# Output projection of images 1 to 3: reordering pixels in TensorE's read of y, or in VectorE's read of PSUM

## The chip, the cores and the metric

The kernel runs on one NeuronCore of a Trainium2 chip. A core has a matrix engine (TensorE, PE in the profile; its weight loads are PEld), VectorE (DVE), ScalarE (ACT), GpSimd (POOL), SyncE (SP, which issues most DMAs), 16 DMA engines, an on-chip memory SBUF, and PSUM, the memory that TensorE writes its results to, in banks of 128 partitions x 512 fp32. [...] The metric is the device time of one execution in microseconds; lower is better.

## The reference, cut to what matters

The input is x, 4 images of 96 channels x 128 x 128 pixels, fp32. Two layers follow one another, each with a residual sum:

```
x = x + L0(group_norm(x))     # layer 0: a four-direction selective scan over 192 inner channels
x = x + L1(group_norm(x))     # layer 1: convolutions whose weights come from an attention product
```

Layer 0 ends in what the change concerns. ym is the sum of the four scans' outputs, 192 channels for each pixel:

```
mu  = yn.mean(-1);  var = yn.var(-1)                       # over the 192 channels of a pixel
yn  = (yn - mu) * rsqrt(var + 1e-5) * ln_w + ln_b
out = einsum('bdhw,cd->bchw', yn, out_w) + out_b           # back to 96 channels
```

Layer 1 begins with a group norm of x + out, so the mean and variance of each channel over all pixels are needed before it starts.

## The kernel before, in words

The program runs in phases. First it projects and convolves x for all four images; beside this run the selective scans (L735 to L854), written to memory as `yms`. Then `ssm_output` (L923) runs for each image: it normalizes, projects and adds the residual, and stores `xnew`. `split_norm` then makes two maps from `xnew`, and the attention of layer 1 follows.

`ssm_output` takes an image in 16 chunks `c` of 1024 pixels (`SN`), each in two halves `h` of 512 (`CH`). Its loop has 18 steps; in each, chunk c is begun (square and sums), chunk c-1 is in the middle (the inverse deviation), and chunk c-2 is finished. The pieces:

- `load_y` (L938): a DMA brings y, 2 x 96 channels x 1024 pixels; three buffers.
- `squares` and `sums` (L942, L949): ScalarE squares y; TensorE sums y and its squares over the channels.
- `rows`, `inverse`, `roots`, `back` (L961 to L987): the sums are copied out of PSUM, spread by small DMAs over 8 partitions (`mq`), turned into 1/sqrt(var + eps), and written to memory (`rd`).
- `spread_out` (L995): a DMA from GpSimd's queue reads `rd` back into `r`, the same row for 96 partitions. ScalarE adds the output bias to the residual `xr` (L1046).
- `projected` (L1005): TensorE multiplies y by `outws`, the output weights with the norm's scale and the mean's removal folded in, into a PSUM bank `po`. fp32 makes two TensorE instructions of each of the two products for a half, so a half has four.
- `scaled`: VectorE multiplies `po` by `r` (L1012), GpSimd adds `xr` (L1015 for images 1 to 3, L1018 for image 0), and VectorE takes the statistics (L1019). A DMA stores the chunk in `xnew` (L1056).

**Pixel order.** Image 0 keeps the pixels of a row in order. Images 1 to 3 (`turned`) store each row of 128 pixels by column mod 4: first the 32 columns 0, 4, 8, ..., then 1, 5, 9, ..., and so on, since the later phases read pixels that way. `turned_view` (L1237) is the view that reads a row in pixel order as if it were stored so: 32 elements at a step of four fp32 (16 bytes), four times. `back` already writes the inverse deviations in the turned order, so `r` is turned. The residual `xr` is in pixel order and is read by GpSimd through the view. In the kernel before, TensorE reads y (its moving operand) through the view too, and `po` is turned.

**The order of work.** Image 0's `ssm_output` runs beside the end of the scans. That of image 1 runs beside `direct_maps` (image 0's convolutions, L2095), and those of images 2 and 3 beside the attention of the image before (`products`, L1469 and L1484; `Taps`, L1635 and L1745). Two generators are woven together by `co_run` (L290): each piece of the main one has a cost, and the other is advanced by as much cost times a pace. For the phases up to the last scan the order of emission is pinned; after it the scheduler orders the instructions. For images 1 to 3 `ssm_output` has two rotating PSUM banks (`psr`), shared by `po` and the sums.

Of the kernel before, what the change touches and what calls it, by code (L numbers as in the profile page):

```python
# [20 lines left out]
CH = 512  # L21
# [9 lines left out]
TW = 4  # L31
NP = TW + 2
TN = W // TW
# [35 lines left out]
def kernel(  # L69
# [26 lines left out]
    nc = tc.nc  # L96
# [184 lines left out]
    def part(ps, *shape):  # L281
        n = 1
        for d in shape[1:]:
            n *= d
        t = bank(ps)[: shape[0], :n]
        return t if len(shape) == 2 else t.rearrange("p (a b) -> p a b", b=shape[2])
# [636 lines left out]
    def ssm_output(b, yms, xnew, stats, ps, side, turned):  # L923
# [5 lines left out]
        with tc.tile_pool(name="c2", bufs=2, side=side) as p2:  # L929
# [3 lines left out]
            ys, sums_of, near, made = {}, {}, {}, {}  # L933
# [64 lines left out]
            def projected(c, h):  # L998
                po = part(ps, C, CH)
                for j in range(2):  # L1000
                    rhs, to = ys[c][:, j, bass.ts(h, CH)], po
                    if turned:
                        rhs = turned_view(rhs)
                        to = po.rearrange("p (h j t) -> p h j t", t=TN, j=TW)
                    nc.tensor.matmul(  # L1005
                        to, lhsT=outws[:, j], rhs=rhs, start=(j == 0), stop=(j == 1)
                    )
                return po

            def scaled(c, h, po):  # L1010
                xr, r = (t[:, bass.ts(h, CH)] for t in near[c])
                nc.vector.tensor_mul(r, po, r)  # L1012
                if turned:
                    v = r.rearrange("p (h j t) -> p h j t", t=TN, j=TW)
                    nc.gpsimd.tensor_add(v, v, turned_view(xr))  # L1015
                    xr = r
                else:
                    nc.gpsimd.tensor_add(xr, r, xr)  # L1018
                nc.vector.bn_stats(stats[:, 2 * c + h], xr)  # L1019

# [3 lines left out]
            for c in range(NS + 2):  # L1024
                new, old = c < NS, c - 2 if c >= 2 else None
                mid = c - 1 if 1 <= c <= NS else None
                if old is not None:
                    po = projected(old, 0)
# [6 lines left out]
                if old is not None:  # L1035
                    scaled(old, 0, po)
                    po = projected(old, 1)
                    ys.pop(old)
# [10 lines left out]
                if old is not None:  # L1049
                    scaled(old, 1, po)  # L1050
                    load_y(c + 1)
# [185 lines left out]
    def turned_view(v):  # L1237

        return v.rearrange("p (h t j) -> p h j t", t=TN, j=TW)
# [1074 lines left out]
    with tc.tile_pool(name="wp", bufs=1, side="left") as wp:  # L2314
# [7 lines left out]
        for images, pace in (([0], 0.25), ([1], 0.75), ([2, 3], 1.35)):  # L2322
            left = projections(images, weights, stats, wp, psl)
            if images[0] == 0:
# [15 lines left out]
                wdt, wbc, outws, outbs = got  # L2340
# [134 lines left out]
```

## Time and profile before

| | us |
|---|---|
| median of 3 runs | 6757.1 (6746.1 to 6758.7) |
| the profiled execution | 6750.3 |
| its span, first to last instruction | 6748.6 |
| busy: TensorE | 5562.2 (82%) |
| busy: VectorE | 4895.1 (73%) |
| busy: ScalarE | 3810.3 (56%) |
| busy: GpSimd | 3441.7 (51%) |
| mean granted TensorE clock | 0.880 of full speed |

The busy shares are means over phases with different limits. In the slices of the page the span is cut in 40 parts of 168.7 us; each digit is a busy share in tenths, and PEclk is the clock that TensorE was granted, in tenths of full speed. `ssm_output` runs from about 2110 to 2370 us for image 0, 3290 to 3600 for image 1, 4050 to 4400 for image 2 and 4960 to 5290 for image 3. A row of the page's groups reads: line, engine, operation, tiles written and read, shape, count; busy time and mean ns of one; idle time of the engine in front of it and what ended that. In a table of stretches each row has the stretch's bounds and length, then each engine's busy us and its number of instructions, the granted clock, the share of DMA time and GB/s. In a timeline a row has the start, the length of a run of like instructions, the engine, the line, and the count.

### The profile page before, as it was taken

Reading aid. Unit: us, or ns where it says so; the run is one execution under the profiler, and the core shown is the slowest. Engines: PE = TensorE matmul, PEld = TensorE weight load, DVE = VectorE, ACT = ScalarE, POOL = GpSimd, SP = SyncE. Lnnn points to the kernel's source line nnn. Section 1 sums busy time; section 2 is a strip of 40 time slices with the busy share of each in tenths; the row PEclk is TensorE's granted clock in tenths of the full one; section 3 lists DMA queues with packets and bytes.
Section 4 is the critical chain, followed back from the end, with each engine's and each line's share of the span. In section 5 each row is a group of like instructions: output and inputs, shape, how many; then the busy total and the mean of one; then the engine's idle time right before and its main releaser. Section 6 shows DMA issues by size and latency. Waiting matters only on the chain. (4 is left out here: it accounts for less than half of the span.)

```text
span 6748.6 us, 76538 instructions
## 1 busy us (share of the span) xinstructions
PE 5562.2 (82%) x23256; PEld 2361.2 (35%) x23256; DVE 4895.1 (73%) x7737; ACT 3810.3 (56%) x4751; POOL 3441.7 (51%) x2683
## 2 busy tenths in 40 slices
PE   6889978878886628999996679977899877878986
PEld 2333323322221104444332243444333454335652
DVE  3247879989896578889646884488874687987657
ACT  1257768777875576676424453475543664544552
POOL 2236758879796438879422353456123475023410
PEclk9999989989997659999997788888988887999997
DMA  7666777866866666766665765555765555865454
GB/s 163 172 159 177 200 216 198 224 177 171 224 180 166 181 191 191 215 182 175 195 163 157 204 166 152 141 150 146 208 189 150 147 147 148 228 181 139 106 146 146
DMA packets 882102, 1176.27 MB, mean 174 GB/s; under 512 B 215230, under 2 KB 740102, under 8 KB 869212
## 3 DMA queue, kind: packets, MB, share of 16 engines
q1 hardware_dynamic: 858076, 1116.43, 61.1%
q0 software_dynamic: 16208, 38.42, 2.0%
q10 hardware_dynamic: 7408, 16.53, 0.8%
q8 instruction: 187, 3.06, 0.2%
q14 instruction: 223, 1.83, 0.1%
HBM read 766.61 MB, written 334.57 MB: 163 GB/s over the span
## 5 line engine op out<-in xcount | busy, mean ns | idle before, releaser
L621 PE MATMUL bank<-y,wp 128*128 128x512 f32 (+3 forms) x3584 | 1320.4, 626 | 81.6 <-DMA y<-y 33.4
L854 POOL TENSOR_TENSOR y<-y,dl 128x1024 f32<-128x1024 f32 x384 | 1054.2, 2745 | 264.1 <-DVE dl L846 232.5
L821 POOL TENSOR_TENSOR dl<-dl,u 128x1024 f32<-128x1024 f32 x384 | 1007.6, 2624 | 223.5 <-ACT dA L797 123.2
L842 DVE TENSOR_TENSOR_SCAN dA<-dA,pBC 128x512 f32<-128x512 f32 x768 | 981.5, 1278 | 30.8
L1469 PE MATMUL two<-ya,wd 128*64 128x192 f32 (+3 forms) x2376 | 601.1, 433 | 172.0 <-ACT odd L1540 98.0
L735 PE MATMUL pBC<-xr,wbc 60*128 60x512 bf16 (+1 forms) x1536 | 455.7, 401 | 329.8 <-DVE dA L842 257.7
L621 PEld LDWEIGHTS bank<-y,wp 128*128 128x128 f32 (+3 forms) x3584 | 459.1, 169 | 753.1 <-issue 657.0
L846 DVE TENSOR_TENSOR dl<-dA,pBC 128x512 f32<-128x512 f32 x768 | 528.2, 688 | 262.3 <-PE pBC L735 189.0
L2095 PE MATMUL bank<-y,wn 128*128 128x384 f32 (+5 forms) x2408 | 683.0, 509 | 36.7 <-DMA y<-x1d 10.7
L1903 ACT COPY yb<-ya 64x768 f32<-64x768 f32 (+1 forms) x660 | 538.1, 815 | 199.2 <-PE two L1469 151.5
L664 ACT ACTIVATE dl<-pd,dtb 128x512 f32<-128x512 f32 x768 | 486.3, 684 | 181.7 <-PE pd L735 172.1
L1469 PE MATMUL two<-yb,wd 128*64 128x192 f32 (+3 forms) x2376 | 575.0, 416 | 0.0
L825 DVE TENSOR_TENSOR pBC<-dl,pBC 128x512 f32<-128x512 f32 x768 | 527.6, 687 | 9.4 <-POOL dl L821 8.5
L1005 PE MATMUL bank<-y,outws 96*96 96x512 f32 x512 | 455.2, 1025 | 1.8 <-DVE r L1012 1.1
L2095 PEld LDWEIGHTS bank<-y,wn 128*128 128x128 f32 (+3 forms) x2408 | 311.8, 169 | 355.4 <-issue 198.8
L1973 POOL COPY own<-ring 32x512 f32<-32x512 f32 (+1 forms) x198 | 218.2, 1137 | 399.0 <-DVE ring L1562 330.1
L797 ACT ACTIVATE dA<-dl,negA 128x1024 f32<-128x1024 f32 x384 | 420.3, 1141 | 2.3
L1469 PEld LDWEIGHTS two<-ya,wd 128*64 128x64 f32 (+1 forms) x2376 | 272.1, 175 | 400.5 <-issue 106.7
L664 ACT ACT_TABLE_LOAD x245 | 314.3, 1283 | 103.3 <-PE pd L735 95.9
L735 PEld LDWEIGHTS <-wbc 60*128 60x128 bf16 (+1 forms) x1536 | 103.3, 96 | 765.8 <-issue 751.8
L1469 PEld LDWEIGHTS two<-yb,wd 128*64 128x64 f32 (+1 forms) x2376 | 298.8, 175 | 160.3 <-issue 52.5
L1469 PE MATMUL two<-ya,wa 128*96 128x384 f32 (+1 forms) x528 | 230.5, 520 | 132.9 <-DMA wd<-wd 86.7
(308 smaller groups left out, 9665.7 us busy)
## 6 DMA issues: line engine op xcount, KB each, us to landing
u<-zb SPq DMA_DIRECT2D x192, 1024.0 KB
yms<-y SPq DMA_DIRECT2D x96, 512.0 KB
y<-yms SPq DMA_DIRECT2D x64, 768.0 KB
xn<-xnew SPq DMA_DIRECT2D x128, 384.0 KB
ya<-vp SPq DMA_DIRECT2D x120, 336.0 KB
y<-y SPq DMA_DIRECT2D x128, 258.2 KB
zb<-z SPq DMA_DIRECT2D x64, 512.0 KB
ya<-x1p SPq DMA_DIRECT2D x90, 336.0 KB
```

Source lines behind the costliest of these rows:

```text
L621: nc.tensor.matmul(blocks(pz[p:e]), lhsT=ws[k][:, d, c : c + e - p], rhs=window(ys[k], at, d, n), start=(i == 0), stop=(i == len(terms) - 1),)
L664: nc.scalar.activation(dst, src, AF.Softplus, bias=bias)
L735: nc.tensor.matmul(p, lhsT=w[rows], rhs=xr[rows, at : at + CH], start=True, stop=True)
L821: nc.gpsimd.tensor_mul(t, t, u_view(n))
L825: nc.vector.tensor_mul(p, live[n]["dl"][:, bass.ts(half, CH)], p)
L842: nc.vector.tensor_tensor_scan(h, h, p, init, ALU.mult, ALU.add)
L846: nc.vector.tensor_mul(live[n]["dl"][:, sl], live[n]["dA"][:, sl], live[n]["C", half])
L854: nc.gpsimd.tensor_add(v, v, t.rearrange("p (a b) -> p a b", b=W))
L1005: nc.tensor.matmul(to, lhsT=outws[:, j], rhs=rhs, start=(j == 0), stop=(j == 1))
L1469: nc.tensor.matmul(of(to[p:e], r), lhsT=w[:, i, c : c + e - p], rhs=tiles(t[k][PAIR[i]][:, SLOT[i]], o, r), start=(k == 0), stop=False,)
L1903: nc.scalar.copy(yb[k][64 * h - 64 : 64 * h, :, :n], ya[k][0:64, :, h * TN : h * TN + n])
L2095: nc.tensor.matmul(pc[p:e, :n].rearrange("p (h w) -> p h w", w=W), lhsT=w[:, c : c + e - p], rhs=v[:, :, 0:W], start=(i == 0), stop=(i == ...
```

## The change

For images 1 to 3, TensorE reads y in pixel order, as for image 0, so `po` is in pixel order. VectorE's multiplication then reads `po` through `turned_view` and writes `r` in place, in turned order. GpSimd's addition and all that follows is as before. Image 0's instructions are unchanged.

```
             def projected(c, h):
                 po = part(ps, C, CH)
                 for j in range(2):
-                    rhs, to = ys[c][:, j, bass.ts(h, CH)], po
-                    if turned:
-                        rhs = turned_view(rhs)
-                        to = po.rearrange("p (h j t) -> p h j t", t=TN, j=TW)
                     nc.tensor.matmul(
-                        to, lhsT=outws[:, j], rhs=rhs, start=(j == 0), stop=(j == 1)
+                        po,
+                        lhsT=outws[:, j],
+                        rhs=ys[c][:, j, bass.ts(h, CH)],
+                        start=(j == 0),
+                        stop=(j == 1),
                     )
                 return po

             def scaled(c, h, po):
                 xr, r = (t[:, bass.ts(h, CH)] for t in near[c])
-                nc.vector.tensor_mul(r, po, r)
                 if turned:
                     v = r.rearrange("p (h j t) -> p h j t", t=TN, j=TW)
+                    nc.vector.tensor_mul(v, turned_view(po), v)
                     nc.gpsimd.tensor_add(v, v, turned_view(xr))
                     xr = r
                 else:
+                    nc.vector.tensor_mul(r, po, r)
                     nc.gpsimd.tensor_add(xr, r, xr)
                 nc.vector.bn_stats(stats[:, 2 * c + h], xr)
```

`turned_view`, which both use, is unchanged:

```
    def turned_view(v):
        return v.rearrange("p (h t j) -> p h j t", t=TN, j=TW)
```

More of the change, by code (lines that the diff above doesn't have):

```diff
@@ L1000, in projected @@
                 for j in range(2):
[L1001 to L1004, printed above, removed]
                     nc.tensor.matmul(
-                        to, lhsT=outws[:, j], rhs=rhs, start=(j == 0), stop=(j == 1)
+                        po,
+                        lhsT=outws[:, j],
+                        rhs=ys[c][:, j, bass.ts(h, CH)],
+                        start=(j == 0),
+                        stop=(j == 1),
                     )
@@ L1011, in scaled @@
                 xr, r = (t[:, bass.ts(h, CH)] for t in near[c])
-                nc.vector.tensor_mul(r, po, r)
                 if turned:
                     v = r.rearrange("p (h j t) -> p h j t", t=TN, j=TW)
+                    nc.vector.tensor_mul(v, turned_view(po), v)
                     nc.gpsimd.tensor_add(v, v, turned_view(xr))
@@ L1017, in scaled @@
                 else:
+                    nc.vector.tensor_mul(r, po, r)
                     nc.gpsimd.tensor_add(xr, r, xr)
```

## The prediction

> **What bounds the kernel now.** I read the page's engine totals first, then the slices, then the stretches in which the changed lines run, and last the single instructions.
>
> ```profile
> PE   6889978878886628999996679977899877878986
> PEclk9999989989997659999997788888988887999997
> ...
> L1005 PE MATMUL bank<-y,outws 96*96 96x512 f32 x512 | 455.2, 1025 | 1.8 <-DVE r L1012 1.1
> ```
>
> Over the whole span no engine is full (TensorE 82%), so the stretch decides. L1005 is the projection: 512 instructions, two per matrix product, of which 128 belong to image 0 and 384 to images 1 to 3. TensorE was idle for only 1.8 us in front of all of them. The next table is busy time by stretch: image 0's normalization, those of images 1, 2 and 3, then (a second answer) a dense stretch of other work.
>
> ```profile
> core 0: us, PE busy (x) PEld busy (x) DVE busy (x) ACT busy (x) POOL busy (x), PEclk, DMA share, GB/s
> 2110.00:2370.00 260.00, 178.06 (x457) 42.17 (x450) 131.34 (x205) 142.20 (x157) 114.91 (x89) 0.67 0.64 182
> 3290.00:3600.00 310.00, 301.08 (x902) 97.94 (x901) 133.89 (x323) 84.22 (x119) 71.33 (x109) 0.93 0.60 160
> 4050.00:4400.00 350.00, 339.64 (x1442) 136.64 (x1442) 162.32 (x323) 144.90 (x190) 134.16 (x165) 0.88 0.55 146
> 4960.00:5290.00 330.00, 319.56 (x1254) 119.42 (x1255) 166.92 (x300) 131.49 (x168) 126.35 (x152) 0.88 0.56 152
> ...
> 2800.00:3250.00 450.00, 414.73 (x1782) 188.03 (x1781) 393.68 (x480) 317.44 (x402) 371.32 (x143) 0.97 0.65 191
> ```
>
> In the three stretches of images 1 to 3, 990 us together, TensorE is busy for 960 us (97%), VectorE for 463, ScalarE for 361, GpSimd for 332; the DMA share is below 0.61. TensorE is the bound there. How much of it the strided projection takes, and whether it is on the chain:
>
> ```profile
> 3290.00:3600.00 310.00, 122.57 (x128) 20.32 (x128) 0.93 0.60 160
> 4050.00:4400.00 350.00, 122.23 (x128) 22.57 (x128) 0.88 0.55 146
> 4960.00:5290.00 330.00, 122.77 (x128) 21.51 (x128) 0.88 0.56 152
> ```
>
> That is 368 us. The chain of waits, cut to 4990 to 5300 us, gives line L1005 34.9%, its largest share. Last, a run of eight of these matmuls in order of time: two of image 0 (contiguous read), then one of image 3 (strided read).
>
> ```profile
> 2253.79 6.80 PE L1005 MATMUL bank<-y,outws 96*96 96x512 f32 x8
> ...
> 2264.13 3.67 PE L1005 MATMUL bank<-y,outws 96*96 96x512 f32 x8
> ...
> 5059.19 7.42 PE L1005 MATMUL bank<-y,outws 96*96 96x512 f32 x8
> ```
>
> Same line, weights and shape. A single matmul lasts about 0.17 us longer than its turn, so one turn is (3.67 - 0.17)/8 = 0.437 us contiguous and (7.42 - 0.17)/8 = 0.906 us strided. The run of 6.80 us is contiguous at half clock: 0.83 us. Strided turns are 0.90 us in both states of the clock.
>
> [...] this trace's clock records in these stretches are 0.5 or 1.0 alone.
>
> **The change part by part.** As built, the changed program has the same instructions in the same order on all five engines, so nothing is moved past a queue and no DMA is added or removed.
>
> *Matmul reads.* 384 instructions go from 0.90 us (346 us in sum) to 0.437 us at full clock (168 us): 178 us less at full clock, but only 384 x 0.05 at half clock. The rest of TensorE's work in the stretches is 960 - 346 = 614 us at a mean clock of 0.896, or 550 us of full-clock work. So the three stretches take 718/(k s) us, where k is the granted clock and s the share in which TensorE is busy. Now they take 990; the change gains 990 - 718/(k s). The output was already written in contiguous order through its view, so that edit costs nothing.
>
> *The share s.* Idle is now 30 us. Part of the strided time is cover: in each half step the squares' sums (L949) wait for ScalarE's square (L942, 1.05 us), with two projection matmuls between (2.02 us at 3402.03). With about 1.05 us of cover left some 0.3 us shows; 96 halves make 29 us. VectorE waited 22.9 us in all for the DMA of r; a shorter step (990/54 = 18.3 us now, 15.9 after) lets this reach TensorE, and I take 10 us. Idle becomes 69 us of some 860: s = 0.92. [...]
>
> *The clock k.* Most half-clock records here follow 7 us in which TensorE was full and the strided matmul held half or more of it, so k should rise if anything; the dense stretch at 2800 without such matmuls has 0.97 at 92% busy. More idle pulls down: stretches at 78 to 81% busy (3790 to 4050, 4450 to 4950, 5650 to 6000) have 0.86 or 0.87. I take 0.91. Then 718/(0.91 x 0.92) = 858 us, a gain of 132.
>
> *The multiplication.* L1012 takes 0.686 us; its read of PSUM now steps by 16 bytes. [...] Above, the nearest rows are these:
>
> ```profile
> L1426 DVE SCALAR_TENSOR_TENSOR diff<-lift 96x128 f32<-96x128 f32 x128 | 45.6, 409 | 7.1 <-POOL lift L1350 6.7
> ...
> L1430 DVE TENSOR_TENSOR pl<-diff 96x128 f32<-96x128 f32 x32 | 9.2, 287 | 3.4 <-DMA vp<-pl 3.4
> ```
>
> L1426 reads two sources at this very step from SBUF and L1430 reads none so: 0.122 us for 128 elements, 0.95 ns each, which makes 0.49 us for 512. [...] VectorE is half idle there, and its cover would be gone only at some 4 us more per multiplication. What it delays directly is the release of a PSUM bank; TensorE and its weight loads waited for that some 12 times of 96 (15 us)[...]. GpSimd's addition and the statistics behind it have idle time on both engines.
>
> **Sum.** The profiled execution took 6750.3 us (span 6748.6), 6.8 us under the median of the runs, 6757.1. Minus 132: 6618 on the profiled one's scale, **6625** on the median's.
>
> **The rivals.**
> *Half of it is eaten by round trips* (0.16). The strided matmuls were padding between squares, row sums, the mq, rd and r DMAs and the multiplication. For: [...] single waits reach 6 to 10 us. Against: image 0's sixteen steps took 15.3 us each (first to last start of L1005, 2121.1 to 2366.3), with no wait of L1012 on a DMA. With s = 0.86 and k = 0.90: 928 us, a gain of 62, 6695.
> *The clock falls and it is slower* (0.05). [...] For: image 0's stretch, 68% busy, was granted 0.67; the one from 2400 to 2800, 66% busy, 0.80. Against: 78 to 81% busy kept 0.86. It decides from k s = 718/990 = 0.725 down. With k = 0.80 and s = 0.86: 1044 us, 54 lost, 6811.
> *The read isn't what makes L1005 slow* (0.03): its turn stays 0.90 us, and the time 6757. Image 0's 0.437 us speaks against it.
>
> **How the numbers follow.** The main case (0.76) runs from k = 0.97, s = 0.95 (779 us, gain 211, 6546) to k = 0.88, s = 0.89 (917, gain 73, 6684). The half-eaten case reaches to a gain of 20. From 6545 to 6720 about 0.17 is left out: the slower case, the null case, and the ends of the others. A measurement can tell some 0.2%, 13.5 us, from no change. Faster by more: 0.76 + 0.15 = 0.91; within: 0.04; slower: 0.05.
>
> **What would show it.** Right: the projection's mean for images 1 to 3 near 0.6 us and its busy time near 190 us instead of 368; the multiplication between 0.69 and 1.18 us; the three stretches near 860 us, TensorE about 92% busy, the clock 0.9 or more, new idle time in front of L949 released by ScalarE's square. Wrong: a projection mean still at 1.08 us; a clock under 0.8 there; a multiplication of several us with TensorE waiting for its bank; or time lost in stretches that hold no projection.

## The result, and the profile after

The changed kernel takes 6666.2 us (median; 6662.8 to 6680.9) against 6752.2 before: a ratio of 0.9877, 95% interval 0.9858 to 0.9896, or 86 us less. The profiled execution has a span of 6663.1 us. The forecast was 6625, with 6545 to 6720 as its range: the sign and the mechanism held, and the gain was about two thirds of the 132 us forecast.

The slices of the page after, to be set against those of before:

```profile
PE   5889978988887626989985579877889777878996
PEclk9999989988997758999997788988879887989987
```

The three stretches, now in 3290 to 3558, 4010 to 4321 and 4880 to 5200 us (bounds and length, busy us and instructions by engine, clock, DMA share, GB/s):

```profile
3290.00:3558.00 268.00, 238.58 (x903) 92.37 (x901) 130.49 (x327) 84.09 (x119) 71.15 (x109) 0.95 0.69 186
4010.00:4321.00 311.00, 281.39 (x1428) 127.83 (x1427) 160.17 (x318) 141.13 (x185) 129.68 (x158) 0.90 0.60 158
4880.00:5200.00 320.00, 277.07 (x1268) 116.05 (x1266) 167.28 (x303) 131.47 (x169) 126.63 (x152) 0.86 0.58 157
```

Their sum went from 990 to 899 us, 91 less; some 5 were given back elsewhere. TensorE's busy time went from 960 to 797 us, 163 less, but its idle time rose from 30 to 102: it is busy for 89% and no longer 97%. By image the stretches are 42, 39 and 10 us shorter, so most of what is missing is missing in image 3. The same stretches for the projection alone (its line is now L1001; the columns are TensorE's busy time, weight loads, clock, DMA share, GB/s):

```profile
3290.00:3558.00 268.00, 63.00 (x128) 18.67 (x128) 0.95 0.69 186
4010.00:4321.00 311.00, 72.92 (x128) 21.75 (x128) 0.90 0.60 158
4880.00:5200.00 320.00, 76.14 (x128) 21.76 (x128) 0.86 0.58 157
```

That is 212 us where it was 368. In order of time, a run of four in image 3 is as short as those of image 0: (1.88 - 0.17)/4 = 0.43 us each.

```profile
5062.63 1.88 PE L1001 MATMUL bank<-y,outws 96*96 96x512 f32 x4
```

The groups of the whole run, by shape, show the multiplication and where TensorE's new idle time stands (after the bar: busy us, mean ns; then idle us before it, and what ended that):

```profile
L949 PE MATMUL bank<-y,mean 96*32 96x512 f32 x512 | 241.0, 726 | 52.4 <-DVE r L1014 32.5 <-DMA y<-yms 14.9 <-ACT st L961 5.0
L949 PE MATMUL bank<-sq,mean 96*32 96x512 f32 x512 | 168.0, 737 | 52.3 <-ACT sq L942 51.7
L1014 DVE TENSOR_TENSOR r<-bank,r 96x512 f32<-96x512 f32 x96 | 63.3, 672 | 124.6 <-DMA r<-rd 56.9 <-PE bank L1001 29.7 <-issue 22.8
```

The same groups before:

```profile
L949 PE MATMUL bank<-y,mean 96*32 96x512 f32 x512 | 222.8, 700 | 17.4 <-DMA y<-yms 8.9 <-ACT st L961 4.4 <-DVE r L1012 4.0
L949 PE MATMUL bank<-sq,mean 96*32 96x512 f32 x512 | 160.9, 709 | 49.8 <-ACT sq L942 49.7
L1012 DVE TENSOR_TENSOR r<-bank,r 96x512 f32<-96x512 f32 x128 | 85.8, 675 | 135.3 <-PE bank L1005 106.6 <-DMA r<-rd 22.9 <-PE bank L949 5.5
```

The multiplication takes 0.672 us with its strided PSUM read, as much as before (0.675, image 0 counted in). In front of it VectorE now waits 56.9 us for the DMA of r (22.9 before), and TensorE's sums wait 32.5 us for the multiplication to free a PSUM bank (4.0 before). The wait for the square hardly grew (49.7 to 51.7).

### The profile page after: what moved, and what is told of

Its sections match the earlier page's. It is cut to its first block, busy times and chain, and to the rows that moved or that the text cites. A ratio compares the mean times of both kernels' runs of the same rounds, so it can differ in the third digit from the quotient of the medians.

```text
span 6663.1 us, 76540 instructions
## 1 busy us (share of the span) xinstructions
PE 5393.7 (81%) x23256; PEld 2343.1 (35%) x23256; DVE 4885.0 (73%) x7737; ACT 3810.5 (57%) x4751; POOL 3437.4 (52%) x2683
## 5 line engine op out<-in xcount | busy, mean ns | idle before, releaser
L1470 PE MATMUL two<-ya,wd 128*64 128x192 f32 (+3 forms) x2376 | 590.5, 426 | 189.5 <-ACT odd L1541 106.6
L1470 PE MATMUL two<-yb,wd 128*64 128x192 f32 (+3 forms) x2376 | 565.2, 410 | 0.0
L1470 PEld LDWEIGHTS two<-ya,wd 128*64 128x64 f32 (+1 forms) x2376 | 267.1, 172 | 394.8 <-ACT odd L1541 115.3
L1470 PEld LDWEIGHTS two<-yb,wd 128*64 128x64 f32 (+1 forms) x2376 | 293.5, 172 | 151.5 <-issue 43.2
L1470 PE MATMUL two<-ya,wa 128*96 128x384 f32 (+1 forms) x528 | 228.7, 516 | 132.7 <-DMA wa<-watd 86.3
L1001 PE MATMUL bank<-y,outws 96*96 96x512 f32 x512 | 296.7, 710 | 3.5 <-DVE r L1014 2.3
```

The source lines that it names most:

```text
L1470: nc.tensor.matmul(of(to[p:e], r), lhsT=w[:, i, c : c + e - p], rhs=tiles(t[k][PAIR[i]][:, SLOT[i]], o, r), start=(k == 0), stop=False,)
```

## The experiments

Ratios are to the kernel before, with 95% intervals. Each group of runs has its own runs of the kernel before (medians of 6745.8 to 6755.3 us), so two runs that are compared with each other can differ by some 10 us more or less by their ratios than by their medians. By the traces, the change and the first three experiments leave the order of the instructions on every engine as it was: in the traces before and after, ScalarE's 4751, VectorE's 7737 and GpSimd's 2683 recorded instructions start in one and the same order, though VectorE's wait for r grew from 22.9 to 56.9 us. From e4 on the scheduler orders part of them anew, so those runs hold a change of order too.

**Where the step costs.** Three kernels put the reordering elsewhere, or shorten its step. The single projection matmuls, image 0's 128 among them (ns, the shortest, the middle and the longest), in the kernel before, the changed kernel, e2 and e3:

```profile
L1005 PE MATMUL bank<-y,outws x512: 592/1078/1196, 2121.1 to 5279.7; 96*96 96x512 f32 x171
L1001 PE MATMUL bank<-y,outws x512: 590/592/1169, 2124.5 to 5177.7; 96*96 96x512 f32 x171
L1005 PE MATMUL bank<-y,outws x512: 589/593/1170, 2127.6 to 5202.0; 96*96 96x512 f32 x171
L1005 PE MATMUL bank<-y,outws x512: 592/612/1170, 2119.2 to 5177.2; 96*96 96x512 f32 x171
```

*e1_view_only*: the kernel before, with VectorE's read alone changed.

```
-                nc.vector.tensor_mul(r, po, r)
+                nc.vector.tensor_mul(v, turned_view(po), v)     # images 1 to 3
```

> One half of the change alone: TensorE still reads y through the strided view, as before, and only VectorE's multiplication reads PSUM through the view (the pixels of images 1 to 3 so come out in another order; timing alone is wanted). Theory (the strided PSUM read is free on VectorE): the multiplication stays at 0.67 to 0.69 us and the ratio to before is 1.000 within 0.2%. Rival (the read costs, and is part of what was lost against the forecast): the multiplication takes 0.8 us or more, and the ratio is 1.001 to 1.005.

Measured: 6753.3 us, ratio 0.9999 (0.9988 to 1.001); the multiplication has a mean of 676 ns. The theory holds: VectorE's multiplication reads fp32 from PSUM at a 16-byte step in the time of the contiguous read (675 ns). The prediction had allowed up to 0.49 us more for each; it is 1 ns.

```profile
L1014 DVE TENSOR_TENSOR r<-bank,r 96x512 f32<-96x512 f32 x96 | 64.3, 676 | 132.4 <-PE bank L1005 100.5 <-DMA r<-rd 23.9 <-issue 6.9
```

*e2_strided_write*: TensorE reads in order, and writes PSUM with a step.

```
-                        rhs = turned_view(rhs)
-                        to = po.rearrange("p (h j t) -> p h j t", t=TN, j=TW)
+                        rhs = rhs.rearrange("p (h t j) -> p h t j", t=TN, j=TW)
+                        to = po.rearrange("p (h j t) -> p h t j", t=TN, j=TW)
```

> The reordering in a third place: TensorE reads y in pixel order and writes PSUM at the 16-byte step; VectorE reads PSUM in order. Theory (only the moving operand's read from SBUF is slow at this step): the projection's turn is 0.437 us at full clock, as in the changed kernel, and the ratio to before is 0.986 to 0.989. Rival [...]: turn 0.85 to 0.91 us, ratio 1.000.

Measured: 6678.8 us, ratio 0.9881 (0.9864 to 0.9897); turns of 0.43 us at full clock. The step of this write is not the 16 bytes that the expectation names: in the order `h t j` consecutive elements lie TN = 32 fp32, or 128 bytes, apart. At that step the write costs nothing in these matmuls (0.43 us, as in the changed kernel), and the rival, that a write with a step takes as long as the slow read (0.85 to 0.91 us), falls for it; a 16-byte step wasn't tried there.

*e3_step_two*: the kernel before with a step of two elements.

```
-                        rhs = turned_view(rhs)
-                        to = po.rearrange("p (h j t) -> p h j t", t=TN, j=TW)
+                        rhs = rhs.rearrange("p (h t j) -> p h j t", t=64, j=2)
+                        to = po.rearrange("p (h j t) -> p h j t", t=64, j=2)
```

> The kernel before, but TensorE reads y at a step of two fp32 (8 bytes) in place of four (16 bytes)[...] (the pixels of images 1 to 3 come out in another order). [...] the turn falls to 0.437 us at full clock and the ratio to before is 0.986 to 0.990. Rival (any step over one is slow): turn stays 0.90 us, ratio 1.000.

Measured: 6674.5 us, ratio 0.9877 (0.9862 to 0.9893); turns of 0.45 us at full clock. A step of 8 bytes is nearly as good as none (0.43 us), a step of 16 bytes is not (0.90 us). Why the two differ isn't shown by these runs. With e2 this also answers the rival that the read isn't what makes the projection slow.

**Where the missing gain went.**

*e4_r_at_once*: r without its round trip.

```
-                near[c] = xr, to
+                near[c] = xr, rs[bass.ts(c, SN)]      # a constant row, written ahead
```

> The changed kernel, but r of images 1 to 3 is read by the same DMA from a constant row in memory, so it no longer waits for the inverse deviation's round trip (the normalization's scale is left out of the output; all instructions stay). Theory (the gain fell short because r comes late, VectorE's multiplication then holds the PSUM bank, and TensorE's sums L949 wait for the bank): VectorE's wait for r falls from 57 us to under 10, TensorE's wait of L949 for the multiplication from 32 us to under 10, and the time falls by 20 to 40 us, ratio to before 0.981 to 0.985. Rival (the rest is lost to the clock, to squares and to the attention's own waits; r only shares the idle time): those two waits shrink, but the time falls by under 8 us, ratio 0.986 to 0.989.

Measured: 6626.9 us, ratio 0.9807 (0.9792 to 0.9821), 39 us less than the changed kernel by the medians, 47 by the ratios. Its stretches, and its groups of the sums and of the multiplication (here L954 and L1019):

```profile
3290.00:3565.00 275.00, 249.70 (x916) 95.95 (x914) 134.39 (x335) 84.22 (x120) 73.58 (x115) 0.91 0.69 182
4010.00:4312.00 302.00, 271.44 (x1430) 124.37 (x1428) 161.49 (x315) 141.44 (x186) 134.44 (x165) 0.93 0.63 167
4880.00:5172.00 292.00, 268.19 (x1296) 117.50 (x1294) 168.02 (x316) 132.84 (x173) 126.74 (x152) 0.91 0.65 173
```

```profile
L954 PE MATMUL bank<-y,mean 96*32 96x512 f32 x512 | 234.1, 711 | 31.8 <-DMA y<-yms 14.3 <-DVE r L1019 13.0 <-ACT st L966 4.4
L1019 DVE TENSOR_TENSOR r<-bank,r 96x512 f32<-96x512 f32 x96 | 63.6, 668 | 77.7 <-DMA r<-rs 21.5 <-PE two L1490 15.5 <-issue 14.3
```

Together 869 us, TensorE idle for 80 of them. VectorE's wait for r is 21.5 us, and TensorE's sums wait 13.0 us for the multiplication: both fell, but not to under 10, and the gain is at the upper end of the theory's or above it. Of the 30 us fewer in the stretches image 3 has 28 and image 2 has 9; image 1 is 7 longer. In the stretches TensorE's waits for the multiplication fall from 35 to 18 us, while those for the square rise from 17 to 26. So a late r is the largest part of the missing gain that a run here took away. How much of the 39 us is r's wait alone isn't shown: image 3 also has a higher clock (0.91 for 0.86), and 222 of VectorE's 7740 instructions stand at another place than in the changed kernel. What the DMA engines move in the stretches is as in the changed kernel, so it is not their load. The trace shows why r is late. From the copy of the sums (L961) to the first multiplication of the chunk 22 to 25 us pass on average in images 1 to 3 before the change, and 20 to 24 after: the small DMAs, VectorE's and ScalarE's few operations and the landings of rd and r (on average 3.5 to 4.0 us and 4.3 to 5.5 us) hardly shorten with the projection. The step went from 18.3 to 16.6 us (899/54). Between the landing of r and its multiplication 3.0 to 4.0 us were left before, 1.7 to 2.6 after. In 10 of the 48 chunks the multiplication started within 0.2 us of the landing before, in 25 after.

*e5_own_banks*: a bank for the projection, a bank for the sums.

```
-                po = part(ps, C, CH)
+                po = ps.tile([128, CH], F32, name="po", tag="po" if turned else "bank")[:C]
...
+                        tc.tile_pool(name="psn", bufs=1, space=PSUM, side="right")
```

> The changed kernel, with the two PSUM banks of images 1 to 3 told apart: one for the projection, one for the sums, in place of two that rotate among both (the normalization, the split and the output each open their own pool for that). r is as late as in the changed kernel. Theory (a late r costs because the sums of the next chunk rotate onto the bank that the waiting multiplication holds): TensorE's wait of L949 for the multiplication falls from 32 us to under 8, and the time by 15 to 35 us, ratio to before 0.982 to 0.985. Rival (a late r costs through VectorE's queue, in which all behind the multiplication waits, whatever the banks): L949's wait moves to the projection L1001 or to other lines, and the ratio stays 0.986 to 0.989.

Measured: 6681.2 us, ratio 0.991 (0.9893 to 0.9926): no gain over the changed kernel, and by the ratios some 22 us slower. Its largest new wait of TensorE (us in total, times, longest):

```profile
PE po L1001 <- DVE r L1014: 82.9, 34, 7.7
```

The sums no longer wait for the multiplication at all, but the projection waits for the multiplication, mostly that of the second half for the first half's (75 of the 83 us). The theory falls in so far as the sums' rotation onto that bank is where the wait shows, not its cause; the rival's half, that the wait moves, is what happened, and its time was missed too.

*e7_banks_one*: image 1's normalization rotates among three banks of its own in place of the two.

```
-        imgs[1].norm(yms[0][1], psr, "right"),
+        imgs[1].norm(yms[0][1], more.enter_context(
+            tc.tile_pool(name="psm", bufs=3, space=PSUM, side="right")), "right"),
```

> The changed kernel with three more PSUM banks for image 1's normalization alone (there is room for them in that stretch), images 2 and 3 as they are. Theory of the bank: in the stretch of image 1 the 10 us of waits of L949 for the multiplication go, in images 2 and 3 they stay; the time falls by 5 to 14 us, ratio to before 0.9855 to 0.987. Rival (VectorE's queue): no change of the stretch, ratio 0.987 to 0.989.

Measured: 6662.2 us, ratio 0.9875 (0.986 to 0.9889): no gain. TensorE's waits in its stretch of image 1:

```profile
PE bank L949 <- ACT sq L942: 12.2, 10, 3.0
PE bank L949 <- DMA y<-yms: 6.7, 3, 2.6
```

The changed kernel has 10.3 us there for the multiplication, 4.6 for the square and 3.3 for y. With the banks the first is gone, and the other two have grown to take its place. The wait did as the theory said and the time as the rival said.

**The squares.** The prediction had set 29 us for squares that lose their cover.

*e6_two_squares*: the changed kernel, and *e9_squares_before*: the kernel before, with the same edit.

```
-                sq = p2.tile([C, SN], F32, name="sq", bufs=1)
+                sq = p2.tile([C, SN], F32, name="sq", bufs=1 + turned)
```

> The changed kernel with two buffers for ScalarE's squares in images 1 to 3 instead of one, so the second half's square need not wait for the first half's sums. Theory of the prediction (part of the cover that the strided matmul gave was for this square): TensorE's wait of L949 for the square (52 us over the whole run, 17 us of it in the three stretches) falls by 10 us or more and the time by 8 to 20 us, ratio to before 0.9845 to 0.9865. Rival (the square is late by ScalarE's own queue, not by its buffer): under 5 us, ratio 0.987 to 0.989.

> The kernel before (TensorE reads y through the strided view) with two buffers for the squares of images 1 to 3. Theory (the second buffer pays in the changed kernel because the strided matmuls no longer cover the wait for the square): with that cover still there it gains under 10 us, ratio to before 0.9985 to 1.001. Rival (the second buffer gives another order of the work that is better whatever the projection reads): 25 to 40 us, ratio 0.994 to 0.996.

Measured: 6629.7 us, ratio 0.9824 (0.981 to 0.9837), for the first; 6710.4 us, ratio 0.9954 (0.9937 to 0.9972), for the second. The edit gains 36 us with the change and about 31 without it. So it is no repair of a cover that the change took away: the rival holds, and the change is worth the same with it (0.9824/0.9954 = 0.987). Some 20 us of what it gains show in the sums' own busy time on TensorE, L949 alone by stretch; before, then with the edit on it (its stretches are other ones, but hold all 256 instructions):

```profile
3290.00:3600.00 310.00, 51.19 (x256) 7.88 (x256) 0.93 0.60 160
4050.00:4400.00 350.00, 47.98 (x256) 6.87 (x256) 0.88 0.55 146
4960.00:5290.00 330.00, 53.54 (x256) 8.21 (x256) 0.88 0.56 152
```

```profile
3290.00:3600.00 310.00, 44.52 (x256) 7.47 (x256) 0.89 0.59 163
4030.00:4370.00 340.00, 43.38 (x256) 7.09 (x256) 0.90 0.56 152
4930.00:5260.00 330.00, 44.88 (x256) 8.05 (x256) 0.88 0.58 158
```

153 us become 133. In the timeline four of these matmuls, each with 32 output columns, start within 0.03 us of each other when y and its square are both at hand, and take 0.6 us together at full clock (at 3364.18 us in the kernel before); two of y alone take 1.0 us (at 3365.06). That more of them run abreast when the square is early is read from the traces, not tried apart. The same table gives 171 us for the changed kernel and 149 for e6: the second buffer takes 20 to 22 us off with and without the change, and the change adds 16 to 18 us whether there are one or two buffers. Why it adds them isn't shown.

*e8_banks_squares*: both edits, of e5 and e6.

> Both: a PSUM bank each for projection and sums, and two buffers for the squares. Theory: the gains add up, since one ends the wait for the multiplication and the other that for the square: 25 to 50 us less than the changed kernel, ratio to before 0.980 to 0.984. Rival: when the one wait goes, the other takes its place, and the time is that of the better of the two alone, within 8 us.

Measured: 6669.5 us, ratio 0.9887 (0.9872 to 0.9902). Neither theory nor rival: the single bank of the projection costs (87.8 us of waits of L1001 for the multiplication) about what the squares gain.

*e10_r_and_squares*: the edits of e4 and e6 together.

> The changed kernel with r read from a constant row, so that it waits for nothing (the normalization's scale is left out of the output), and two buffers for the squares. Theory (late r and late square are two separate losses in the three stretches, about 40 and 36 us): they add in the main, 6580 to 6605 us, ratio to before 0.975 to 0.978. Rival (each is only the wait that ends last, and the other takes its place): 6615 to 6630 us, ratio 0.979 to 0.982.

Measured: 6602.9 us, ratio 0.9795 (0.9775 to 0.9816). The time lies in the theory's span and the ratio in the rival's. By the medians they gave 39 and 36 us alone and 63 together; by the ratios 47, 36 and 55. So of e6's 36 us some 24 or some 8 add to e4's gain, and these runs don't tell the theory from the rival.

**Making r less late.** Both start from e6.

*e11_later*: the projection stands one sub-step later, after the inverse of the next chunk, and the first half's multiplication and the second half's projection follow one sub-step later too.

```
-                if old is not None:
+                if old is not None and not turned:
                     po = projected(old, 0)
                 yield 1.2
...
+                if old is not None and turned:
+                    po = projected(old, 0)
```

> The changed kernel with two buffers for the squares, and the projection of images 1 to 3 stands one sub-step later in each step, so r has 1.4 of the step's 8.2 units of time more, some 2.5 us (y is released later by as much). Theory (the round trip of r, 20 to 24 us from the sums to the multiplication, is what is late next): VectorE's wait for r falls from 79 us to under 50 and the time to 6600 to 6622 us, ratio to before 0.978 to 0.981. Rival (y is then late instead): ScalarE's wait for y rises over 60 us, the time stays at 6625 us or more.

Measured: 6637.0 us, ratio 0.9849 (0.9829 to 0.9869). VectorE's wait for r fell from e6's 79.3 us to 22.9, but TensorE's projection now waits 30.5 us for the multiplication, and ScalarE's wait for y rose from 41.9 to 50.4. No gain over e6: the rival has the time, but y is not the whole of its reason.

*e12_r_sooner*: the DMA of r right behind that of rd.

```
                 if mid is not None:
                     back(mid)
+                    if turned:
+                        spread_out(mid)
```

> The changed kernel with two buffers for the squares, and the DMA of r stands right behind the write of the inverse deviations instead of one sub-step later. Theory: the time from the landing of rd to the issue of r (1.5 to 2.6 us on average) falls by about 1 us, and with it the time by 5 to 12 us, 6617 to 6625 us. Rival (GpSimd's queue then waits for rd with its additions behind it): no gain or slower, 6630 us or more.

Measured: 6624.8 us, ratio 0.9823 (0.9802 to 0.9844): as e6. The time from rd's landing to r's issue stayed at 1.6 to 2.4 us. The trace says why: the instructions stand in e6's order on every engine, but for one of the 48 DMAs of r, which comes one place sooner; the scheduler had put the others back. So this run tests neither the theory nor the rival; it is in effect e6 measured a second time. This kernel is the fastest that computes the whole of the reference, and both times it beats the changed kernel.

## Why the prediction was right in sign and too large in size

**The bound and the formula.** That TensorE bounds the three stretches, and that they take 718/(k s) us, held: with the measured clock k = 0.901 (the three rows, weighted by length) and busy share s = 797/899 = 0.887 the formula gives 898 us, and 899 were measured. The gain per matmul, 0.906 to 0.437 us, was found as read from image 0. The projection's busy time was not: 212 us, where 190 were foreseen. The prediction counted its matmuls by their turns (346 us before, where 368 are busy), and what they last beyond it stood among the rest of TensorE's work; it is about as much after as before, so the sum came out all the same.

**The clock.** 0.91 was forecast, 0.901 found: about 8 us of the 41 by which 899 exceeds 858. By image it was 0.95 (0.93 before), 0.90 (0.88) and 0.86 (0.88). The half-clock moments that the prediction spoke of did go. In the three stretches before, 22 of the trace's 29 half-clock records (times in which TensorE was granted half the clock, the shortest of them 3.41 us; the 22 make 126 us) follow 7 us in which TensorE was over 99% busy, with 47 to 87% of that time in the strided projection; after the change there is none of this kind. The other kind, after 7 us with gaps, grew from 7 records (82 us) to 21 (188 us), 92 us of it in image 3. The prediction had weighed one against the other in its 0.91, but for less idle time than came. e1, which keeps the strided read, has 21 records of the first kind; e2 and e3, which don't, have none.

**The share s is the step that failed.** Idle time was to be 69 us and is 102: some 32 us of the 41. The terms of that sum were mis-sized both ways. For r's DMA 10 us were set: TensorE's waits for the multiplication grew from 5 to 35 us (10.3, 13.2 and 8.9 us before L949, 2.3 before L1001), and the run without r's round trip gained 39 us (e4). For the squares 29 us were set: that wait, which was to be the new idle time, grew only from 10.7 to 16.6, and the loss that a second buffer repairs was there before the change (e9). For waits of the main work, convolutions and attention, none was set; TensorE's waits in these stretches hold about 30 us of them now (L1470 and L1636 on VectorE the most) where there were some 10, 23 of them in image 3. Waits for y grew from 2 to 8 us. Prices for waits were taken from how long the cover was, and not from how much of r's chain of 20 to 25 us a shorter step still holds.

**The multiplication.** The bounds for its extra cost were 0 and 0.49 us, the upper one an estimate from two groups that read SBUF (L1426 and L1430, 409 and 287 ns for 128 elements), not PSUM; where between them it would lie no run had shown. The cost is 0 (e1: 676 ns against 675), the lower bound. It changed nothing in the sum, and VectorE had room for the upper bound too (96 x 0.49 = 47 us, beside 463 of the 990 us before).

**The rivals.** That half would be eaten by round trips (6695) was nearer to the truth than the main case, in its time (29 us off, not 41) and in part of its cause: r, squares and y do wait, and s of 0.887 lies between its 0.86 and the main case's 0.92. The clock did not fall on the whole (0.896 and 0.901 in the stretches), and the read was what made the projection slow (e2, e3).

**Open.** How much of the gain of e6 is the order and how much the packing of the sums isn't settled, nor how much of e4's is the order and the clock. Why idle time and half clock gather in image 3 isn't either; the runs with the same order (e2, e3) show it too. A pipeline one step deeper, which would give r a whole step more, wasn't tried.

## What to carry to other kernels

Look at the step of a matmul's moving operand in bytes: in this fp32 kernel 16 bytes doubled the matmul's time at full clock (0.90 for 0.43 us), 8 bytes did not (0.45), and the same reordering was free in the PSUM write (0.43 us, e2) and in VectorE's PSUM read (676 ns against 675, e1). When the bound engine is relieved, the loops beside it can keep their length (r's 22 to 25 us became 20 to 24, while the step went from 18.3 to 16.6): compare each round trip with the new, shorter step before counting the whole saving. Before a run is read as a test of an edit, compare the order of instructions in its trace with that of the run it is set against: e12's was e6's. And a wait that ends last need not be alone: with the bank's 10.3 us gone (e7), the square's went from 4.6 to 12.2 us and y's from 3.3 to 6.7.

## What the runs showed of the hardware

An fp32 moving operand at a 16-byte step takes 0.90 us for 512 columns at full and at half clock alike (the middle of 221 and of 46 successive pairs in the kernel before), while a contiguous one goes from 0.43 to 0.85 us; so the strided one loses most when the clock is high. At an 8-byte step it takes 0.45 us at full clock. A matmul's PSUM write at a 128-byte step cost nothing (0.43 us), nor did VectorE's read of PSUM at a 16-byte step (672 and 676 ns against 675). A TensorE that was busy without a gap was still granted the half clock where strided matmuls held 47 to 87% of the 7 us ahead: 22 of 29 half-clock records in the three stretches before, none of 21 after.
